# A graph kernel's last stretch in another order: preparation in four sorts instead of five, layers begun two sorts sooner, row fetches put behind the tails' scatters

## The chip, the cores and the metric

The kernel runs on one core of a Trainium2 chip. Its time is the device time of one execution in microseconds. Of the kernel before, nine executions were timed; a tenth was profiled, and that one gives the trace from which all durations are taken.

The engines are TensorE (matmuls; PE in the profile, PEld its weight loads), VectorE (DVE), ScalarE (ACT), GpSimd (POOL) and SyncE (SP). Each works through its own queue in the order in which the program issued it. Transfers are issued from SP's and POOL's queues.

## The reference

Sixteen graphs of 1024 nodes, 64 channels each, and a 0/1 adjacency. Two layers, each on a layer norm, each added to `x`:

```python
# layer 0: h = max(layernorm(x), 0)
skip = jnp.maximum(jnp.where(nb > 10, (nb + 1) // 2, 1), 1)
rem = neigh & (sk > 1) & (rank % sk == sk - 1) & mask[:, :, None]
rem = rem | jnp.swapaxes(rem, 1, 2)
nd = jnp.where(rem, 0.0, adj_) > 0
s = jnp.sort(jnp.where(nd[..., None], x[:, None, :, :], jnp.inf), axis=2)
agg = sum of 0.25, 0.5, 0.25 times the quantiles 0.25, 0.5, 0.75 of s   # per node and channel
out = x + agg; y = relu(out @ W1 + b1) @ W2 + b2                        # masked, x + y
# layer 1: h = max(layernorm(x), 0)
x1 = bn(relu(adj @ (h @ W) + b))      # three times, x1, x2, x3
x + relu(concat([x1, x2, x3]) @ Wl + bl)
```

So each node's remaining neighbours are sorted channel by channel, three weighted quantiles make its aggregate, and then come three products with the whole adjacency.

## The kernel before, in words

The graphs are worked in eight pairs, `p` = 0 to 7. The 1024 nodes of a graph are ordered by their number of neighbours and cut into blocks, so that every block has a sorting network of its own length.

**Blocks.** Three wide blocks (0, 1, 2 in `BLOCKS`, called so here) are gathered on TensorE (`gather_block`: VectorE makes one-hot selections `s`, L1245, TensorE multiplies them with the features into `pg`, L1270, ScalarE copies the result to `g`, L1274) and sorted by `sort_block`. The middle block (`MID`, nodes 960 to 1008) is gathered in the same way and sorted by `sort_pairs`, for two pairs in one network. The last sixteen nodes of each graph, the tails, are sorted for four pairs at once (`TAILS`: after pair 4's turn, and for pairs 4 to 7 in the late part). Three blocks of nodes (`NODES`: 17, 19 and 21 neighbour slots) are sorted by `sort_nodes`. Their rows are not gathered by products: `fetch_nodes` fetches them from `rows_d`, one slot of one graph at a time, with an indirect transfer from POOL's queue (`ask`, L1486), followed after the second graph's by a small memset on POOL (L1498, a "rest"). The first graph's fetch also waits until the sort at that place has gone on. The first and second node block are fetched for one pair, the third for two pairs; `NODE_ORDER` is the order of these jobs. Their buffer, tag "gn", exists once; two late jobs have buffers of their own.

All the sorts are VectorE's compare steps (L1186), the weights and sums follow at L1198 and L1207. The aggregates go to HBM (`agg_d`) by indirect transfers from POOL's queue (`scatter`, L1368).

**Preparation.** `prepare(p)` works out which neighbours remain: ScalarE's and TensorE's passes over the adjacency; `above` and `place` (L975); POOL's scatters to `live_d` (L983) and their load `lp` (L998); ScalarE's `liveT` and `listed` (L1063); then VectorE's `top` (L779, eight neighbours at a time), `rows_listed` (L799), `z` and the features `hp` (L764 to 767). It is done for the second graph after the first.

**Weaving.** The order on the engines is written out: `weave(sort, others...)` runs a sort's generator and steps the others when their share of the sort is passed. `asking(job, first, end, share)` spreads a share of a job's fetches over a stretch of the sort; what is left is issued when that job's sort begins (`ask.rest()`). `steps(n)` gives out `SHARES[n]` steps of the preparation, or in the late part `LATE_SHARES[n]` steps of `later`. A generator that is done simply takes no more steps.

In the loop, the turn of pair `p` has five sorts with preparation of pair `p + 1` beside them: block 0, a job of nodes, block 1, block 2, and one more job of nodes. Then come the middle block of `p` and `p + 1`, with block 0 of `p + 1` gathered beside it, and the next turn. After pair 6's turn the late part sorts pair 7: block 0, a job of nodes (the third node block of pairs 4 and 5), block 1, block 2, the next job of nodes, the tails, a job of nodes, the middle block of pair 7, and three jobs of nodes.

**Layers.** `later` runs the second part of every pair beside the late sorts. `load(p)` (SP, L1693 to 1702) loads `x`, `h`, the aggregates and the mask; the aggregates' load waits for all scatters to that pair's `agg_d`. `first` adds the aggregates (L1594), multiplies by the two weight matrices (`pm` L1603, `py` L1607) and makes the layer norm (`agg`, L624 to 632). `second` loads the transposed adjacency (`adjT`, L1715, two of 1 MB) and runs the three graph layers: the weights' product (`xw`, L1636 to 1642), the product with the adjacency in 96 matmuls (`pg`, L1652), `xT` (L1656), the output's product `pf` (L1668) and the result (L1672 to 1677). In

```python
        loaded = load(p + 1)
        for _ in range(5):
            now.step()
            yield
        ahead = Steps(first(*loaded))
        while now.step():
            yield
            if ahead is not None and ahead.step():
                yield
```

the next pair's load is issued, five more steps of the present pair are taken, and then its first layer alternates with the present pair's steps. `done.sent` says up to which pair the scatters have been issued; `load` may go no further.

Of the kernel before, what the change touches and what calls it, by code (L numbers as in the profile page):

```python
# [30 lines left out]
TAUS = ((0.25, 0.25), (0.5, 0.5), (0.75, 0.25))  # L31

SHARES = (20, 22, 14, 30, 9)
LATE_SHARES = (8, 8, 8, 8, 9, 9, 10, 8, 11, 8, 8)

MAGIC = 8388608.0

# [372 lines left out]
def graph_layers_kernel(ctx: ExitStack, tc: tile.TileContext, ins, out: bass.AP):  # L410
# [6 lines left out]
    NP = NB // 2  # L417
# [1108 lines left out]
    def asking(fetched, first, end, share=1.0):  # L1526

        return fetched[4], math.ceil(share * NODES[fetched[1]][3]), first, end
# [151 lines left out]
    def later(pools, keep, done):  # L1680
# [41 lines left out]
        for p in range(NP):  # L1722
            now = Steps(second(p, *given))
            now.step()
            yield
            ahead = None
            if p + 1 < NP:
                loaded = load(p + 1)
                for _ in range(5):
                    now.step()  # L1730
                    yield
                ahead = Steps(first(*loaded))
# [4 lines that stand above are left out]
            if ahead is not None:  # L1737
                ahead.rest()
                given = ahead.result
# [146 lines left out]
    with ExitStack() as stack:  # L1886
# [6 lines left out]
        with ExitStack() as inner:  # L1893
# [11 lines left out]
            def fetch_next(tag="gn"):  # L1905
                pairs, i = next(jobs)
                return fetch_nodes([sts[p] for p in pairs], i, pools, tag)
# [5 lines left out]
            for p in range(NP - 1):  # L1913
                st = sts[p]
                ahead = Steps(prepare(p + 1, early))

                def steps(n):
                    return ahead, SHARES[n], 0.0, 1.0

                weave(sort_block(st, 0, pools), gather_block(st, 1, pools), asking(nodes, 0.0, 0.9), steps(0))  # L1920
                weave(sort_nodes(nodes, pools), gather_block(st, 2, pools), steps(1))
                nodes = fetch_next()
                weave(sort_block(st, 1, pools), asking(nodes, 0.1, 1.0, 0.4), steps(2))
                send_nodes()
                both = rows_of_pairs(MID, p, p + 1, p, pools, "g1")
                weave(
                    sort_block(st, 2, pools), gather_block(st, MID, pools, into=both),
                    gather_block(st, MID + 1, pools, (early[0], "a", 2)), asking(nodes, 0.0, 0.7), steps(3),
                )
                if p in TAILS:  # L1930
                    tails = rows_of_pairs(MID + 1, *TAILS[p], TAILS[p][1], pools, "g0")
                weave(sort_nodes(nodes, pools), steps(4))
                ahead.rest()
                sts.append(ahead.result)
                nodes = fetch_next()
                if p in TAILS:
                    weave(sort_pairs(MID + 1, *TAILS[p], tails, pools))
                    send(pools)
                weave(
                    sort_pairs(MID, p, p + 1, both, pools), gather_block(sts[-1], 0, pools, first=0.3, end=1.0),  # L1940
                    asking(nodes, 0.0, 1.0, 0.4),
                )


        with ExitStack() as inner:
# [5 lines left out]
            def steps(n):  # L1951
                return ahead, LATE_SHARES[n], 0.0, 1.0

            st = sts[-1]
            weave(sort_block(st, 0, pools), gather_block(st, 1, pools), asking(nodes, 0.0, 0.9), steps(0))
            weave(sort_nodes(nodes, pools), gather_block(st, 2, pools), steps(1))
            nodes = fetch_next()
            then = [fetch_next("r0")]
            weave(sort_block(st, 1, pools), asking(nodes, 0.0, 0.9), steps(2))
            send_nodes()  # L1960
            both = rows_of_pairs(MID, NP - 1, NP, NP - 1, pools, "g1")
            weave(
                sort_block(st, 2, pools), gather_block(st, MID, pools, into=both), asking(then[0], 0.0, 0.9), steps(3)
            )
            tails = rows_of_pairs(MID + 1, *TAILS[NP - 1], NP - 1, pools, "g0")
            weave(sort_nodes(nodes, pools), gather_block(st, MID + 1, pools, into=tails[:, :, -TW:]), steps(4))
            then += [fetch_next(), fetch_next("s"), fetch_next("s")]
            weave(
                sort_pairs(MID + 1, *TAILS[NP - 1], tails, pools), asking(then[1], 0.0, 0.9), steps(5),
            )  # L1970
            send(pools)
            sent_ahead[0] = last_sent[0]
            done.sent = NP - 2
            weave(sort_nodes(then[0], pools), asking(then[2], 0.1, 1.0, 0.6), steps(6))
            send_nodes()
            weave(sort_pairs(MID, NP - 1, NP, both, pools), asking(then[2], 0.0, 0.8), asking(then[3], 0.8, 1.0, 0.1), steps(7))
            send(pools)
            weave(sort_nodes(then[1], pools), asking(then[3], 0.0, 1.0, 0.5), steps(8))
            send_nodes()
            done.sent = NP - 1  # L1980
            weave(sort_nodes(then[2], pools), asking(then[3], 0.0, 0.9), steps(9))
            send_nodes()
            weave(sort_nodes(then[3], pools), steps(10))
            send(pools)
            done.sent = NP
            ahead.rest()
# [49 lines left out]
```

## Time and profile before

| | us |
|---|---|
| median of 9 executions | 2853.47 |
| lowest, highest | 2831.88, 2862.99 |
| profiled execution | 2835.27 |
| its span | 2833.5 |
| VectorE busy in it | 2343.4 (83%) |
| TensorE busy | 2149.8 (76%) |
| POOL busy | 1710.0 (60%) |
| ScalarE busy | 1619.8 (57%) |

The page gives each engine's busy time, its busy share in 40 slices of the span (a digit is tenths), and the costliest groups of instructions: line, engine, operation, tiles, count, then busy time, mean nanoseconds of one, and the idle time ahead of them with what ended it. Beside it the trace was asked for stretches of the span: for each its length, then each engine's busy time with the number of instructions in brackets, the clock that TensorE was granted, the share of the transfer engines and GB/s. In the timeline a line has start, duration, engine, line, operation, tiles, number of instructions, and in square brackets the idle time before it and what ended it. A stall is read from that bracket, not from the busy share.

The last sorts lie in the span as follows, each ending where the next begins: second node block of pair 5, 2051.6 to 2087.8; middle block of pairs 6 and 7, with what follows it, to 2153.2; block 0 of pair 7 to 2196.9; third node block of pairs 4 and 5 to 2246.1; block 1 to 2285.5; block 2 to 2343.9; first node block of pair 6 to 2409.6; tails to 2484.5; then second node block of pair 6 (fetched earlier into its own buffer) to 2563.9; middle block of pair 7 to 2603.1; third node block of pairs 6 and 7 to 2652.2; the two node jobs of pair 7 to 2685.2 and 2726.3. The layers alone go on to 2833.5.

### The profile page before, as it was taken

To read this page: it belongs to the slowest core of one execution; us is meant where nothing else is said; L and a number is where in the kernel's file an instruction comes from. 1 tells how busy PE (TensorE), PEld (TensorE's weight loads), DVE (VectorE), ACT (ScalarE), POOL (GpSimd) and SP (SyncE) were. 2 spreads that over 40 slices of the span, in tenths; PEclk is the share of its full clock that TensorE was granted. 3 is DMA by queue.
4 is the path that set the end of the run, shared out by engine and by line. 5 is a ranking of instruction groups with operands and counts; after the bars stand their busy time and mean duration, and the time that the engine had idled before them with its cause. 6 is when DMAs were issued, how large, how long until landed. Compare 5 with 4: busy or idle time off the path is not lost. (4 is left out here: it accounts for less than half of the span.)

```text
span 2833.5 us, 54810 instructions
## 1 busy us (share of the span) xinstructions
PE 2149.8 (76%) x21204; PEld 1383.0 (49%) x21220; DVE 2343.4 (83%) x5452; ACT 1619.8 (57%) x3255; POOL 1710.0 (60%) x1570
## 2 busy tenths in 40 slices
PE   4658976796689578868975588679758998748888
PEld 2425544454455445545652355445535555425555
DVE  6358988798899888898979998889886987949963
ACT  4564768476758666686767267667672332303322
POOL 7225764575838673865476748674867288888300
PEclk9869977897799789978986799789978988869999
DMA  5114122222322132314152032132213135213221
GB/s 157 53 45 134 59 74 67 87 64 69 76 83 78 56 83 74 90 53 124 55 84 60 21 107 89 47 96 74 80 48 76 22 77 92 60 33 75 70 61 46
DMA packets 262765, 205.43 MB, mean 73 GB/s; under 512 B 218720, under 2 KB 219104, under 8 KB 258400
## 3 DMA queue, kind: packets, MB, share of 16 engines
q1 hardware_dynamic: 178528, 133.61, 16.1%
q0 software_dynamic: 40960, 62.37, 8.9%
q10 hardware_dynamic: 43008, 5.87, 1.8%
q8 instruction: 168, 2.75, 0.4%
q14 instruction: 101, 0.83, 0.1%
HBM read 148.89 MB, written 52.81 MB: 71 GB/s over the span
## 5 line engine op out<-in xcount | busy, mean ns | idle before, releaser
L1486 POOL DMA_INDIRECT g_nodes<-rows_d,rows_listed x744 | 969.2, 1303 | 713.9 <-DVE prod L1198 260.3
L1270 PE MATMUL pg<-s,hp 128*64 128x496 fp8e4 (+5 forms) x8064 | 753.9, 338 | 146.6 <-DVE s L1245 51.1
L1270 PEld LDWEIGHTS <-hp 128*64 128x64 bf16 x8064 | 458.2, 114 | 385.6 <-ACT hp L764 60.7
L1498 POOL MEMSET rest_row<- 1x768 bf16 x372 | 288.7, 776 | 0.1
L1652 PE MATMUL pg<-adjT,xw 128*64 128x512 fp8e4 x2304 | 280.5, 393 | 9.2 <-ACT xw L1637 5.2
L1245 DVE TENSOR_SCALAR s<-r 128x3200 uint16<-128x3200 uint16 (+2 forms) x192 | 206.9, 1086 | 64.4 <-PE pg L1270 49.0
L983 POOL DMA_INDIRECT live_d<-edge,place x128 | 162.9, 1273 | 127.1 <-DVE place L975 64.5
L1274 ACT ACTIVATE g<-pg 128x400 f32<-128x400 f32 (+3 forms) x168 | 83.9, 499 | 224.2 <-PE pg L1270 150.6
L1652 PEld LDWEIGHTS <-xw 128*64 128x64 bf16 x2304 | 135.0, 113 | 138.9 <-issue 24.1
L850 ACT ACTIVATE edge<-a 128x1024 fp8e4<-128x1024 uint32 x128 | 135.4, 1058 | 99.7 <-DMA a<-in_adj 96.5
L942 ACT ACTIVATE edge<-q,bias 128x1024 fp8e4<-128x1024 f32 x128 | 141.9, 1110 | 59.4 <-PE q L937 55.0
L915 ACT ACTIVATE stays<-cs,back 128x1024 f16<-128x1024 f32 x128 | 138.7, 1113 | 58.2 <-PE cs L911 29.0
L1186 DVE TENSOR_TENSOR t<-g 128x800 f32<-128x800 f32 (+9 forms) x184 | 168.0, 926 | 2.4 <-ACT g L1274 0.4
L1018 PE MATMUL pt<-ident_h,lp 128*128 128x128 bf16 x1024 | 106.8, 274 | 81.2 <-ACT liveT L1024 38.3
L1341 PE MATMUL pg<-s,hp 128*64 128x384 bf16 (+14 forms) x1872 | 152.7, 303 | 14.3 <-DVE s L1310 10.9
L1186 DVE TENSOR_TENSOR g<-t 128x992 f32<-128x992 f32 (+7 forms) x176 | 160.0, 934 | 2.3
L1186 DVE TENSOR_TENSOR t_nodes<-g_nodes 128x256 f32<-128x256 f32 (+6 forms) x192 | 124.5, 658 | 42.5 <-DMA g_nodes<-rows_d,rows_listed 28.6
L969 ACT ACTIVATE stays<-keys,minus 128x1024 fp8e4<-128x1024 f32 x120 | 134.0, 1117 | 43.2 <-PE keys L954 27.7
L1368 POOL DMA_INDIRECT agg_d<-o,node_of x96 | 134.5, 1401 | 28.9 <-issue 25.5
L1310 DVE TENSOR_SCALAR s<-r 128x192 bf16<-128x192 bf16 (+11 forms) x544 | 115.2, 302 | 41.1 <-remote 29.8
L857 PE MATMUL ptE<-ident_h,one 128*128 128x128 bf16 x1024 | 83.8, 231 | 81.0 <-DVE one L854 59.8
L1018 PEld LDWEIGHTS <-lp 128*128 128x128 fp8e4 x1024 | 92.0, 126 | 93.7 <-issue 79.6
(272 smaller groups left out, 5116.4 us busy)
## 6 DMA issues: line engine op xcount, KB each, us to landing
a<-in_adj SPq DMA_DIRECT2D x128, 512.0 KB
lp<-live_d POOLq DMA_DIRECT2D x32, 514.0 KB
adjT_d<-edgeT SPq DMA_DIRECT2D x16, 1024.0 KB
adjT<-adjT_d SPq DMA_DIRECT2D x16, 1024.0 KB
g_nodes<-rows_d,rows_listed POOLq DMA_INDIRECT x744
room<-in_x SPq DMA_DIRECT2D x16, 256.0 KB
h_again<-h_d SPq DMA_DIRECT2D x16, 256.0 KB
xt<-in_x SPq DMA_DIRECT2D x16, 256.0 KB
```

What stands on the lines that cost most here:

```text
L850: nc.scalar.activation(edge[:, t, :N], a[:, :].bitcast(U32), AF.Sign, accum_out=found[:, 0, b, t : t + 1], saturate=False)
L915: nc.scalar.activation(stays[:, t, :], cs, AF.Abs, bias=back[:, t : t + 1], scale=2.0)
L942: nc.scalar.activation(edge[:, t, :N], q, AF.Relu, bias=bias(-2.0), accum_out=nv[:, t : t + 1], saturate=False)
L983: sent = nc.gpsimd.indirect_dma_start(out=live_d[b][:, :], out_offset=bass.IndirectOffsetOnAxis(ap=place[:, t : t + 1], axis=0), in_=edge[ ...
L1018: nc.tensor.matmul(out=pt[:, u, :], lhsT=lp[:, u * P : (u + 1) * P], rhs=ident_h, start=True, stop=True)
L1186: sorted_by[0] = nc.vector.tensor_tensor(view(bufs, o, n1, n2), view(bufs, a, n1, n2), view(bufs, b, n1, n2), ALU.max if op else ALU.min)
L1245: nc.vector.tensor_scalar(s[:, j, :, us, :], st.r[0][:, :, us, j0:j1], abs(k - 3), 0x0808, ALU.logical_shift_right if k > 3 else ALU.logic ...
L1270: summed = nc.tensor.matmul(out=pg[x * C : (x + 1) * C, those, :], lhsT=st.hp[:, part, x, u, :], rhs=picked, start=(i == 0 and part == 0), ...
L1341: summed = nc.tensor.matmul(out=pg[x * C : (x + 1) * C, ks, w0:], lhsT=st.hp[:, part, x, u, :], rhs=s[:, ks, x, u, w0:], start=(whole and ...
L1486: asked = nc.gpsimd.indirect_dma_start(out=g[:, k, a * C : (a + 1) * C], out_offset=None, in_=rows_d[st.p][:, :], in_offset=bass.IndirectO ...
L1498: rested[0] = nc.gpsimd.memset(rest_row, 0.0)
L1652: nc.tensor.matmul(out=pg[cs, :], lhsT=part[:, u, cs], rhs=adjT[x][:, u, sl], start=(u == 0 and k == 0), stop=(u == NT - 1 and k == len(xw ...
```

## The change: what it does

The instructions are the same on every engine, in number and kind. From pair 6's turn on they stand in another order.

- In the turn of pair 6 the 95 steps of preparation go beside four sorts (`LAST_SHARES`), and none beside its fifth sort and the middle block after it; these two leave the loop and stand at the head of the late part, with 6 and 5 steps of the layers beside them. `LATE_SHARES` has 13 entries instead of 11.
- `first(p + 1)` starts after two instead of five more steps of the present pair.
- The third node block of pairs 6 and 7 (`then[1]`): only 0.3 of its fetches are put beside the tails' sort, the rest beside the sort after it, and so behind the tails' scatters in POOL's queue. The fetches of the two jobs after it move back likewise.

```diff
@@ -31,7 +31,8 @@
 TAUS = ((0.25, 0.25), (0.5, 0.5), (0.75, 0.25))
 
 SHARES = (20, 22, 14, 30, 9)
-LATE_SHARES = (8, 8, 8, 8, 9, 9, 10, 8, 11, 8, 8)
+LAST_SHARES = (24, 26, 17, 30)
+LATE_SHARES = (6, 5, 6, 6, 6, 6, 6, 7, 10, 8, 11, 8, 8)
 
 MAGIC = 8388608.0
 
@@ -1726,7 +1727,7 @@
             ahead = None
             if p + 1 < NP:
                 loaded = load(p + 1)
-                for _ in range(5):
+                for _ in range(2):
                     now.step()
                     yield
                 ahead = Steps(first(*loaded))
@@ -1915,7 +1916,7 @@
                 ahead = Steps(prepare(p + 1, early))
 
                 def steps(n):
-                    return ahead, SHARES[n], 0.0, 1.0
+                    return ahead, (SHARES if p < NP - 2 else LAST_SHARES)[n], 0.0, 1.0
 
                 weave(sort_block(st, 0, pools), gather_block(st, 1, pools), asking(nodes, 0.0, 0.9), steps(0))
                 weave(sort_nodes(nodes, pools), gather_block(st, 2, pools), steps(1))
@@ -1929,6 +1930,10 @@
                 )
                 if p in TAILS:
                     tails = rows_of_pairs(MID + 1, *TAILS[p], TAILS[p][1], pools, "g0")
+                if p == NP - 2:
+                    ahead.rest()
+                    sts.append(ahead.result)
+                    break
                 weave(sort_nodes(nodes, pools), steps(4))
                 ahead.rest()
                 sts.append(ahead.result)
@@ -1952,35 +1957,41 @@
                 return ahead, LATE_SHARES[n], 0.0, 1.0
 
             st = sts[-1]
-            weave(sort_block(st, 0, pools), gather_block(st, 1, pools), asking(nodes, 0.0, 0.9), steps(0))
-            weave(sort_nodes(nodes, pools), gather_block(st, 2, pools), steps(1))
+            weave(sort_nodes(nodes, pools), steps(0))
+            nodes = fetch_next()
+            weave(
+                sort_pairs(MID, NP - 2, NP - 1, both, pools), gather_block(st, 0, pools, first=0.3, end=1.0),
+                asking(nodes, 0.0, 1.0, 0.4), steps(1),
+            )
+            weave(sort_block(st, 0, pools), gather_block(st, 1, pools), asking(nodes, 0.0, 0.9), steps(2))
+            weave(sort_nodes(nodes, pools), gather_block(st, 2, pools), steps(3))
             nodes = fetch_next()
             then = [fetch_next("r0")]
-            weave(sort_block(st, 1, pools), asking(nodes, 0.0, 0.9), steps(2))
+            weave(sort_block(st, 1, pools), asking(nodes, 0.0, 0.9), steps(4))
             send_nodes()
             both = rows_of_pairs(MID, NP - 1, NP, NP - 1, pools, "g1")
             weave(
-                sort_block(st, 2, pools), gather_block(st, MID, pools, into=both), asking(then[0], 0.0, 0.9), steps(3)
+                sort_block(st, 2, pools), gather_block(st, MID, pools, into=both), asking(then[0], 0.0, 0.9), steps(5)
             )
             tails = rows_of_pairs(MID + 1, *TAILS[NP - 1], NP - 1, pools, "g0")
-            weave(sort_nodes(nodes, pools), gather_block(st, MID + 1, pools, into=tails[:, :, -TW:]), steps(4))
+            weave(sort_nodes(nodes, pools), gather_block(st, MID + 1, pools, into=tails[:, :, -TW:]), steps(6))
             then += [fetch_next(), fetch_next("s"), fetch_next("s")]
             weave(
-                sort_pairs(MID + 1, *TAILS[NP - 1], tails, pools), asking(then[1], 0.0, 0.9), steps(5),
+                sort_pairs(MID + 1, *TAILS[NP - 1], tails, pools), asking(then[1], 0.0, 0.9, 0.3), steps(7),
             )
             send(pools)
             sent_ahead[0] = last_sent[0]
             done.sent = NP - 2
-            weave(sort_nodes(then[0], pools), asking(then[2], 0.1, 1.0, 0.6), steps(6))
+            weave(sort_nodes(then[0], pools), asking(then[1], 0.1, 1.0), steps(8))
             send_nodes()
-            weave(sort_pairs(MID, NP - 1, NP, both, pools), asking(then[2], 0.0, 0.8), asking(then[3], 0.8, 1.0, 0.1), steps(7))
+            weave(sort_pairs(MID, NP - 1, NP, both, pools), asking(then[2], 0.0, 1.0, 0.6), steps(9))
             send(pools)
-            weave(sort_nodes(then[1], pools), asking(then[3], 0.0, 1.0, 0.5), steps(8))
+            weave(sort_nodes(then[1], pools), asking(then[2], 0.0, 0.5), asking(then[3], 0.5, 1.0, 0.3), steps(10))
             send_nodes()
             done.sent = NP - 1
-            weave(sort_nodes(then[2], pools), asking(then[3], 0.0, 0.9), steps(9))
+            weave(sort_nodes(then[2], pools), asking(then[3], 0.0, 0.9), steps(11))
             send_nodes()
-            weave(sort_nodes(then[3], pools), steps(10))
+            weave(sort_nodes(then[3], pools), steps(12))
             send(pools)
             done.sent = NP
             ahead.rest()
```

## The prediction

> **What bounds the kernel now.** I read the page first, then the stretches of the last 830 us sort by sort, then the waits, and last the timeline around each place that the change touches.
>
> ```profile
> span 2833.5 us, 54810 instructions
> DVE  6358988798899888898979998889886987949963
> POOL 7225764575838673865476748674867288888300
> L1486 POOL DMA_INDIRECT g_nodes<-rows_d,rows_listed x744 | 969.2, 1303 | 713.9 <-DVE prod L1198 260.3
> L1498 POOL MEMSET rest_row<- 1x768 bf16 x372 | 288.7, 776 | 0.1
> ```
>
> VectorE sorts and sets the pace nearly everywhere. The exception is the 4 in its row of slices, five from the end: there VectorE idles while POOL stands at 8. A fetch of rows costs POOL 1.303 us busy, and 0.30 us stands ahead of nearly every one that follows another fetch, so 1.6 us; a rest costs 0.776 + 0.16 = 0.94 us. Sort by sort (length, then PE, PEld, DVE, ACT, POOL busy):
>
> ```profile
> 2051.60:2087.80 36.20, 21.43 (x177) 12.31 (x174) 30.37 (x77) 23.53 (x33) 16.31 (x15) 0.64 0.23 73
> 2087.80:2153.20 65.40, 41.67 (x425) 25.47 (x427) 49.15 (x175) 44.74 (x105) 59.52 (x51) 0.80 0.37 88
> 2153.20:2196.90 43.70, 38.26 (x384) 26.95 (x380) 33.51 (x43) 7.86 (x18) 24.61 (x20) 0.92 0.09 16
> 2285.50:2343.90 58.40, 56.79 (x507) 37.44 (x505) 56.87 (x81) 14.69 (x25) 52.30 (x44) 0.98 0.40 91
> 2343.90:2409.60 65.70, 56.71 (x429) 36.57 (x425) 46.74 (x115) 20.53 (x58) 52.85 (x46) 0.82 0.60 96
> 2409.60:2484.50 74.90, 56.98 (x434) 35.54 (x430) 73.19 (x227) 23.91 (x58) 67.33 (x61) 0.89 0.25 66
> 2484.50:2563.90 79.40, 39.54 (x270) 21.92 (x271) 37.43 (x81) 12.99 (x28) 67.31 (x70) 0.72 0.14 23
> 2726.30:2833.50 107.20, 96.33 (x802) 58.45 (x796) 37.77 (x52) 26.74 (x44) 2.41 (x2) 0.97 0.15 41
> ```
>
> The first two are the last sorts of the loop (second node block of pair 5, middle block of pairs 6 and 7). The tails' sort ends at 2484.5; in the next, VectorE works 37.43 of 79.40 us. After the last sort come 107.2 us in which TensorE (96.33) finishes the layers. The waits of the stretch from 2484.5 say what VectorE lacks, and the timeline says why:
>
> ```profile
> DVE agg L1594 <- issue: 36.3, 1, 36.3
> ```
> ```profile
> 2523.52 0.94 POOL L1486 DMA_INDIRECT g_nodes<-rows_d,rows_listed  x1 [0.30 <-issue]
> 2524.77 0.87 POOL L1368 DMA_INDIRECT agg_d<-o_tails,node_of  x1 [0.31 <-issue]
> 2532.39 1.22 DVE L1594 TENSOR_TENSOR agg<-agg,h_late 128x1024 f32<-128x1024 f32 x1 [36.27 <-issue]
> ```
>
> Pair 4's first layer waits for the aggregates that the tails' scatters write, and the scatters stand in POOL's queue behind fetches: POOL, 40 us late, holds VectorE for 36.3 us. The start of that queue is where the change works first:
>
> ```profile
> 2047.97 0.17 DVE L975 TENSOR_SCALAR place<-above 128x8 int32<-128x8 f32 x1 [0.34 <-issue]
> 2100.77 0.75 DVE L779 MAX8 top<-listed 128x8 f32<-128x256 f32 x2 [1.74 <-ACT listed L1063]
> 2085.30 1.08 POOL L1486 DMA_INDIRECT g_nodes<-rows_d,rows_listed  x1 [14.40 <-DVE t_nodes L1186]
> 2186.41 1.49 DVE L1186 TENSOR_TENSOR t_nodes<-g_nodes 128x1280 f32<-128x1280 f32 x1 [9.81 <-DMA g_nodes<-rows_d,rows_listed]
> 2725.25 10.75 PE L1652 MATMUL pg<-adjT,xw 128*64 128x512 fp8e4 x96
> ```
>
> The second graph's neighbours are listed 53 us after its places are known; 42 fetches start when the node sort has released its buffer (2085.3), and 101 us later VectorE still waits 9.8 us for the last of them.
>
> **The change part by part.** No instruction comes or goes: TensorE, VectorE, ScalarE, POOL and SP issue what they issued, in another order. What counts is what each place waits for now.
>
> *Preparation in four sorts; start of the fetches.* Pair 7's listing (`top` to `hp`, 73 VectorE instructions, 17.8 us) ran inside the pairs' sort of 65.4 us; now it must end with the node sort before it. It cannot start before `listed`, and as VectorE works in order, the sort behind it waits along. The first graph's scatters to `live_d` stand behind 19 fetches of their sort instead of 24, 5 x 1.6 = 8 us sooner, so `place` of the second graph comes at about 2040. From there to `listed` POOL's 11 more scatters, two loads and ScalarE's `liveT` took 53 us here and 45 in two earlier turns; I take 49: 2089 instead of 2100. The 17.8 us of listing, of which a few are done beside the wait, and about 10 of sort and `hp` follow: the node sort ends near 2115, and its buffer is released 24 us later than before, at 2109. Bounds: +15 (45 us, listing half hidden) and +37 (`listed` no sooner than before and everything after it).
>
> *From there to the end of the third node block of pairs 4 and 5* (2246.1 before). The same 42 fetches, with 6 scatters among them instead of 8 (2 x 1.4 = 3 us less). VectorE is no cover lost: between the two places it worked 49.2 + 33.5 of 109.1 us, and the listing's 17.8 are gone from it, so it waits for the fetches as it did, 9.8 us before, more now. Behind the last fetch 7 layer instructions fewer stand (17 instead of 24), at 0.7 to 1.2 us each 7 us. **+24 - 3 - 7 = +14 us** (+5 to +27). The layer steps given to the loop's last two sorts (16 VectorE instructions) are paid here, in sorts that wait anyway: no cost of their own, up to 10 us if the wait is gone.
>
> *From there to the tails' scatters* (2524.8, 278.7 us). POOL is the bound: it had no break over 4 us in it. After the change 113 fetches stand in it where 128 stood, since 15 of the third block's fetches move behind the scatters; rests 71 for 72, scatters 14 in both. 15 x 1.6 + 0.9 = 25, and of the 4.0 us break (at 2405.6) I take 3 as gone, as VectorE comes sooner: **-28 us**. Bounds: -18 (15 x 0.95 + 0.30 = 1.25 us each, the pace of the line at 2523.52) and -36 (with the one fetch of 8.6 us too). The wait for the aggregates therefore does not go: VectorE too gets there sooner, by the 16 to 18 layer instructions already done and fewer waits in the sorts from 2285.5 on. I expect 25 to 33 us of the 36.3 to remain.
>
> *The scatters themselves.* Pair 4's two were first and second of eight; now first and seventh. Five more at 1.14 us each (0.84 + 0.30 in this block): **+6 us** (0 to +9).
>
> *From pair 4's first layer to the last sort's end* (2532.4 to 2726.3, 193.9 us, VectorE full but for short breaks). Between the two, 24 VectorE instructions fewer stand in the queue, as the layers are at another place: at the stage's mean 0.45 us that is 11, at 0.68, as a layer's, 16; I take **-13**. Against it: 69 fetches instead of 54 stand behind the scatters, 24 us of POOL. The cover is POOL's idle time there, 22.5 us ahead of the scatter at 2685.6 and about 18 in the sort before it; it just suffices. SP's queue is crossed too: the load of the next pair's aggregates, which waits for the third block's scatters, now stands ahead of the load of `adjT`. Without cover these give up to 13 back: -17 to 0.
>
> Together the last sort ends at 14 - 28 + 6 - 13 = **21 us sooner, near 2705.**
>
> *The tail.* The layers give up their lead: at the tails' sort 108 of their VectorE instructions are done where 111 were, at the last sort 206 where 212 were. Pair 6's last product began 1.05 us before the last sort ended (2725.25); now pair 5's third layer still stands there, as the first layer of the next pair is pulled ahead of it by three steps: one `pg` pass of 10.75 us, about half of an output product of 5.62, the weights' product 2: **+15 us** on the 107.2, in which TensorE is 96.33 busy and hides nothing. Bounds +6 (half runs in VectorE's gaps) and +22 (the loads of `adjT` late as well).
>
> Sum: **-6 us**. The profiled execution took 2835.27 around its span of 2833.5, so it would take 2829; against the median of 2853.47, which lies 0.64% above that execution, **2847 us**. The five terms' bounds, taken as independent, make +-18 us; eight in ten within +-13.
>
> [...] Fetches take 0.95 us busy where VectorE idles (2523.52) and 1.303 in the mean. [...]
>
> **The rivals.**
> *The stall goes.* If the listing ends with the sort at 2100 (+5 instead of +14), the fetches keep 1.25 to 1.6 us and the tail grows by 8 only: 5 - 30 + 6 - 14 + 8 = -25, 2828 us. For it: the idle 65 - 49 us of VectorE in the pairs' sort. Against: the chain to `listed` was 45 us or more in every turn.
> *The layers fall behind (slower).* The tail takes pair 5's third layer, +15 to +22, and POOL pays the sooner scatters back in the two sorts after them, so that the last sort ends where it did: 2869 to 2875, say 2871. It decides from the point where the last sort gains under the tail's 15 us, and is over 0.5% once it gains under 1. For it: TensorE 96.33 of 107.2, and the cover of the 24 us is used up. Against: 15 fetches did leave the path.
> *Nothing moves*: POOL's total is the same and the fetches only change places, 2853.
>
> **How the numbers follow.** Forecast 0.45, the stall goes 0.27, the layers fall behind 0.23, nothing 0.05. 0.5% is 14 us (2839 and 2868), about what can be told from no change. The forecast's own range 2834 to 2860 gives 0.13 faster, 0.31 same, 0.01 slower; the first rival 0.25 and 0.02; the second 0.02 same, 0.21 slower; the third 0.05 same. Faster 0.38, same 0.40, slower 0.22. Range: 2820 to 2872, from the first rival less 8 to the second.
>
> **What would show it.** Right: 42 fetches starting near 2109, that block's end near 2260, the first tails' scatter near 2510, a wait of 25 to 33 us at `agg`, the last sort's end near 2705, a tail of some 122. Wrong: `listed` no sooner than 2100; POOL waiting between loop end and tails' scatters, so that asks weren't the bound; VectorE waiting for rows in the last two sorts; a tail under 113.

## The result and the profile after

The changed kernel is slower: 2909.06 us in the median (2895.24 to 2927.64) against 2849.72 for the kernel before (2824.86 to 2875.1), ratio 1.0219 with a 95% interval of 1.0191 to 1.0247. Forecast was 2847, with 2820 to 2872 as the range. The two profiled executions lie further apart than the medians, 2919.93 against 2835.27 us.

The page of the changed kernel, and its sorts by stretches with the columns of before:

```profile
span 2918.2 us, 54787 instructions
DVE  6358988788888979889989997896897987847852
POOL 7234856484828655773857666738474687977200
L1487 POOL DMA_INDIRECT g_nodes<-rows_d,rows_listed x744 | 1004.1, 1350 | 763.3 <-DVE prod L1199 273.4
```
```profile
2090.30:2138.40 48.10, 22.42 (x197) 13.55 (x198) 45.71 (x137) 36.89 (x63) 5.52 (x1) 0.75 0.06 12
2397.30:2453.20 55.90, 36.18 (x320) 24.76 (x319) 37.49 (x84) 14.64 (x44) 36.61 (x30) 0.88 0.51 84
2453.20:2518.30 65.10, 37.38 (x268) 23.88 (x265) 64.10 (x216) 17.09 (x48) 61.10 (x39) 0.78 0.17 51
2518.30:2607.40 89.10, 39.44 (x259) 22.83 (x260) 37.42 (x80) 12.88 (x29) 71.41 (x72) 0.68 0.18 34
2790.30:2918.20 127.90, 112.17 (x906) 71.52 (x902) 41.71 (x59) 29.15 (x47) 1.97 (x2) 0.96 0.19 55
```

VectorE's work is the same (2342.8 us), its dip five slices from the end is still there. The loop's last node sort takes 48.1 us for 36.2, the tail 127.9 for 107.2. POOL, which was expected to be the bound between loop and tails' scatters, works only 36.61 of 55.9 us in the first node block of pair 6. The wait at the first layer of pair 4, from the list of waits in 2518.3 to 2607.4, has grown:

```profile
DVE agg L1595 <- DMA agg<-agg_d: 44.8, 1, 44.8
```

And the timeline at the places that the prediction named:

```profile
2111.67 0.75 DVE L780 MAX8 top<-listed 128x8 f32<-128x256 f32 x2 [2.25 <-ACT listed L1064]
2132.88 10.81 POOL L1487 DMA_INDIRECT g_nodes<-rows_d,rows_listed  x1 [52.53 <-DVE t_nodes L1187]
2231.16 1.49 DVE L1187 TENSOR_TENSOR t_nodes<-g_nodes 128x1280 f32<-128x1280 f32 x1 [20.35 <-DMA g_nodes<-rows_d,rows_listed]
2429.56 0.69 DVE L1643 TENSOR_TENSOR xw<-rest,xw 128x512 bf16<-128x512 f32 x1 [12.83 <-ACT none L1331]
2447.69 2.06 POOL L1487 DMA_INDIRECT g_nodes<-rows_d,rows_listed  x1 [12.45 <-DVE prod L1199]
2570.70 0.87 POOL L1369 DMA_INDIRECT agg_d<-o_tails,node_of  x1 [0.30 <-issue]
```

The 42 fetches start 47.6 us later than before, VectorE waits 20 us for the last of them, later 12.8 us behind ScalarE, and POOL then 12.5 us behind VectorE. The first tails' scatter comes 45.9 us later instead of 15 sooner. Two of the signs that were named for a wrong forecast are there: the second graph's listing begins no sooner than 2100 (at 2111.7), and POOL waits between the loop's end and the tails' scatters.

Cut at the five places of the prediction, the profiles give this. The first row goes to the end of the second sort of pair 6's turn; at the end of the sorts that the change leaves alone, two sorts earlier, its two numbers are +7.9 and -5.2. The last column sets the whole change against the fetches' part alone on two chips of like pace (runs e5_again and e13_fetch2 below), so it is what the first two parts cost.

| | forecast | after less before | whole change less fetches' part |
|---|---|---|---|
| ahead of block 1's sort in pair 6's turn | 0 | +10.9 | -2.9 |
| to the end of the third node block of pairs 4 and 5 | +14 | +29.8 | +23.7 |
| from there to the first tails' scatter | -28 | +5.2 | +15.1 |
| from there to pair 4's first layer | +6 | +7.2 | +2.5 |
| from there to the last sort's end | -13 | +10.9 | +7.7 |
| the tail | +15 | +20.7 | +17.8 |
| sum | -6 | +84.7 | +63.9 |

### The profile page after: what moved, and what is told of

Read it like the earlier page. It is cut to its first block, busy times and chain, and to the rows that moved or that the text cites. A ratio compares the mean times of both kernels' runs of the same rounds, so it can differ in the third digit from the quotient of the medians.

```text
span 2918.2 us, 54787 instructions
## 1 busy us (share of the span) xinstructions
PE 2173.2 (74%) x21204; PEld 1399.2 (48%) x21220; DVE 2342.8 (80%) x5452; ACT 1620.0 (56%) x3255; POOL 1737.4 (60%) x1570
## 5 line engine op out<-in xcount | busy, mean ns | idle before, releaser
L1487 POOL DMA_INDIRECT g_nodes<-rows_d,rows_listed x744 | 1004.1, 1350 | 763.3 <-DVE prod L1199 273.4
L1271 PE MATMUL pg<-s,hp 128*64 128x496 fp8e4 (+5 forms) x8064 | 765.2, 339 | 153.9 <-DVE s L1246 53.2
L1653 PE MATMUL pg<-adjT,xw 128*64 128x512 fp8e4 x2304 | 289.3, 400 | 14.6 <-issue 6.3
L984 POOL DMA_INDIRECT live_d<-edge,place x128 | 157.0, 1227 | 124.7 <-DVE place L976 63.3
L1653 PEld LDWEIGHTS <-xw 128*64 128x64 bf16 x2304 | 143.0, 115 | 144.6 <-issue 41.4
L970 ACT ACTIVATE stays<-keys,minus 128x1024 fp8e4<-128x1024 f32 x120 | 134.1, 1118 | 44.8 <-PE keys L955 27.0
L1657 ACT ACTIVATE xT<-pg,c_L_gnn_b 128x512 f32<-128x512 f32 x48 | 32.8, 684 | 198.0 <-PE pg L1653 161.5
```

The source lines that it names most:

```text
L984: sent = nc.gpsimd.indirect_dma_start(out=live_d[b][:, :], out_offset=bass.IndirectOffsetOnAxis(ap=place[:, t : t + 1], axis=0), in_=edge[ ...
L1271: summed = nc.tensor.matmul(out=pg[x * C : (x + 1) * C, those, :], lhsT=st.hp[:, part, x, u, :], rhs=picked, start=(i == 0 and part == 0), ...
L1487: asked = nc.gpsimd.indirect_dma_start(out=g[:, k, a * C : (a + 1) * C], out_offset=None, in_=rows_d[st.p][:, :], in_offset=bass.IndirectO ...
L1653: nc.tensor.matmul(out=pg[cs, :], lhsT=part[:, u, cs], rhs=adjT[x][:, u, sl], start=(u == 0 and k == 0), stop=(u == NT - 1 and k == len(xw ...
```

## The experiments

**Each part alone.** The four kernels ran on one chip, whose median for the kernel before is 2774.97.

Only the fetches (the last hunks of the diff):

```diff
-                sort_pairs(MID + 1, *TAILS[NP - 1], tails, pools), asking(then[1], 0.0, 0.9), steps(5),
+                sort_pairs(MID + 1, *TAILS[NP - 1], tails, pools), asking(then[1], 0.0, 0.9, 0.3), steps(5),
...
-            weave(sort_nodes(then[0], pools), asking(then[2], 0.1, 1.0, 0.6), steps(6))
+            weave(sort_nodes(then[0], pools), asking(then[1], 0.1, 1.0), steps(6))
...
```

> Only the third part of the change: the fetches of the third node block of pairs 6 and 7 move behind the tails' scatters; preparation stays in five sorts, the layers' shares and the five steps stay. Theory (the loss comes from the preparation in four sorts, the fetches are not to blame): 15 fetches at 1.6 us leave POOL's queue ahead of the scatters, the first tails' scatter comes near 2502 instead of 2524.8, the wait at the first layer of pair 4 falls from 36 to about 15 us, and the kernel is 5 to 20 us faster than before. Rival (the fetches that moved back hold up the later sorts): VectorE waits for rows in the last three sorts, and the kernel is 5 to 20 us slower.

2753.74 us, ratio 0.9916 (0.9888 to 0.9945): faster. The stretch to the tails' scatters is 262.1 us (267.1 and 263.6 in two later profiles of the same kernel), 12 to 17 shorter than in the profile of before, and the wait at pair 4's first layer 21.8 us. The tail is unchanged, 107.0.

Only the sooner first layer:

```diff
-                for _ in range(5):
+                for _ in range(2):
                     now.step()
```

> Only the second part: the next pair's first layer begins after two instead of five more steps. Theory: the tail is what it touches, a part of pair 5's third layer slips behind the last sort: +5 to +15 us, all of it after the last sort's end. Rival (the order of SP's loads holds up the layers beside the sorts): the same or more, but lost before the last sort's end. Second rival: nothing, within 5 us.

2793.33 us, ratio 1.0074 (1.0045 to 1.0104). The tail is 115.0, so 8 us are lost there; the rest is lost earlier, and the longest waits there are not for SP's loads. In the first node block's sort of pair 6 (list of waits, 2269 to 2345):

```profile
ACT o L1389 <- DMA agg_d<-o,node_of: 29.8, 1, 29.8
DVE xT L1657 <- ACT xT L1656: 24.1, 2, 23.6
```

`o` is the buffer from which a block's aggregates are scattered. There are three; the fourth copy on ScalarE waits for the first scatter, the scatter stands in POOL's queue behind fetches, and VectorE's next layer step stands behind ScalarE. In the kernel before that copy waited 2.0 us. A layer step that comes sooner comes to this place before POOL does.

Preparation in four sorts with the layers begun sooner, fetches and five steps as before (first and last hunks of the diff without the `range` and `asking` lines):

> Only the first part: preparation in four sorts and the layers begun beside the loop's last two sorts with the new shares; fetches and the five steps as before. Theory (preparation in four sorts loses the time): the sort of block 2 in the last turn starts some 25 us late, the node sort after it ends some 38 us late, and the kernel is 35 to 65 us slower, the larger part of the whole change's 59. Rival (it is the three together, or the other two): within 15 us of before.

2819.31 us, ratio 1.0161 (1.0122 to 1.0199). Counted from the sorts ahead of it, and against the first profile of before, block 2's sort starts 15 us late (25 were expected), the node sort after it ends 27 us late (38 expected). The tail is 120.8.

The same without layer steps in the loop's last two sorts:

```diff
-LATE_SHARES = (6, 5, 6, 6, 6, 6, 6, 7, 10, 8, 11, 8, 8)
+LATE_SHARES = (0, 0, 8, 8, 8, 8, 9, 9, 10, 8, 11, 8, 8)
```

> Preparation in four sorts alone: the last two sorts of the loop have no steps of the layers beside them, the later shares, the fetches and the five steps are those of before. Theory: as slow as the kernel with the layers begun sooner, within 10 us, since the delay arises in the preparation and the layer steps lie beside waits. Rival (the layer steps put in the two sorts hold up the listing, TensorE and ScalarE being in order): 15 us or more faster than that kernel, and the node sort after block 2 ends 10 us sooner than there.

2801.95 us, ratio 1.0091 (1.0054 to 1.0127). So preparation in four sorts costs 27 us and the layers 17 more, against the theory; but the rival's reason is not it either, since the node sort ends 28 us late here too. The layer steps pay at the third node block (it ends 10 us late with them, 24 without), and lose the same in the tail (120.8 against 106.4). In between, the stretch from the third node block to the tails' scatters takes 304.7 us with them and 289.2 without, so that the scatters come no sooner: POOL's fetches take 9 us longer (189.0 for 179.9, 129 each), VectorE's longest wait in the sort before the tails' is 21.0 for 10.4 us, and POOL's longest wait for a fetch buffer, first with the layer steps, then without:

```profile
POOL g_nodes L1487 <- DVE prod L1199: 10.8, 1, 10.8
```
```profile
POOL g_nodes L1487 <- DVE prod L1199: 3.9, 1, 3.9
```

The two kernels differ in `LATE_SHARES` alone and ran on one chip, so this is shown by an edit: layer steps that come sooner make this stretch longer, in VectorE and in POOL. Where the 17 us of the medians arise is open; the two profiled executions lie only 6 us apart (2811.34 and 2805.57).

**Do the parts add up?** On a chip with 2770.67 for before:

> The changed kernel once more, on the chip on which its parts are measured. The three parts alone gave 1.6%, 0.7% and -0.8%. Theory (the parts add up): 1.5% slower, and no wait of ScalarE of 7 us before block 2's sort nor of VectorE of 11 us in the third node block's sort, which only that one profile showed. Rival (the third part loses its gain beside the others): 2.0 to 2.5% slower, as measured before.

2813.38 us, ratio 1.0166 (1.0126 to 1.0206). The parts alone give 1.61 + 0.74 - 0.84 = 1.5%: they add up. The two long waits named there are absent. The interval of the first measurement (from 1.0191) just meets this one (to 1.0206); what it may owe to its chip comes below.

Without the fetches' part:

> The changed kernel with the fetches where they were: first and second part together. Theory (parts add up): 2.3% slower, and the fetches' part is worth 0.8% here too. Rival (first and second part let VectorE run into POOL sooner, so that what the fetches' order gains is lost in other waits): 1.5 to 2.2% slower, no more than 0.3% from the changed kernel.

2834.24 us, ratio 1.0235 (1.0193 to 1.0277). So the fetches' part is worth 0.7% beside the others too: the first tails' scatter comes 303.8 us after the third node block without it and 282.1 with it. From the lists of waits of this kernel, and of the changed one on the same chip:

```profile
DVE agg L1595 <- DMA agg<-agg_d: 67.8, 1, 67.8
```
```profile
DVE agg L1595 <- DMA agg<-agg_d: 46.7, 1, 46.7
```

An edit of the preparation's shares:

```diff
-LAST_SHARES = (24, 26, 17, 30)
+LAST_SHARES = (24, 26, 6, 41)
```

> The changed kernel with the preparation's steps in its last turn given as 24, 26, 6 and 41 instead of 24, 26, 17 and 30: at the end of block 1's sort 56 steps are out, as in the kernel before. Theory (the chain of the second graph, put ahead of the last gather of block 2 on TensorE and ScalarE, delays that sort): block 2's sort starts within 5 us of the kernel before, 15 to 25 us sooner than in the changed kernel, the node sort after it ends as late as there or up to 10 us sooner since it waits for the listing, and the kernel is 0 to 15 us faster than the changed one. Rival (the listing is only pushed back): the node sort ends 10 us or more later than in the changed kernel, and the kernel is 10 us or more slower.

2814.86 us, ratio 1.0173. The edit left the order of the instructions as it was: in the traces it is the same on VectorE, POOL and SP, and on ScalarE and TensorE a few neighbours at one place are exchanged. So it tells nothing of the theory and only repeats the changed kernel. That the second graph's chain ahead of the last gather delays block 2's sort is therefore read from the trace, not shown by an edit.

**Is POOL's queue the bound?** Fetches' part, and no rests in the late part (`done` is made where the late part begins):

```diff
+    resting = [True]
...
-                    if a == G - 1:
+                    if a == G - 1 and resting[0]:
...
             done.sent = 4
+            resting[0] = False
```

> The fetches' part alone, and in the late part no rests between the fetches: some 92 memsets of 0.94 us leave POOL's queue, 73 of them between the third node block of pairs 4 and 5 and the tails' scatters. Theory (POOL's queue is what sets the end): the tails' scatters come 40 to 65 us sooner, the wait at the first layer of pair 4 goes, and the kernel is another 15 to 35 us faster than with the fetches' part alone, that is 1.4 to 2.1% faster than before. Rival (the rests pace the transfers, without them the fetches take longer): a fetch takes 0.3 us or more longer in the mean, and the kernel is within 10 us of the fetches' part alone, or slower.

2710.43 us, ratio 0.9802 (0.9761 to 0.9843), faster than both kernels. The stretch to the tails' scatters is 237.2 us, the wait at the first layer of pair 4 is gone. On the two chips that ran the fetches' part with and without these rests (below), the stretch is 31 and 28 us shorter without them, while the 73 rests in it took POOL 54 us. So POOL's queue sets much of the length of this stretch, but not all of it. Four more kernels, no rests in the late part of the changed kernel, half of a block's fetches put later in it, no rests in the late part of the kernel before, and none in the whole kernel with the fetches' part, ran together on a chip with 2864.05 for before:

> The changed kernel without rests between the fetches of the late part. Theory (in the changed kernel VectorE runs into POOL's queue, at the copies for block 2's scatters and at the first layer of pair 4; what is left without that is a later loop end, some 20 us, and a longer tail, some 18): both waits go, the kernel is 60 to 90 us faster than the changed one, and still 25 to 45 us slower than the fetches' part without rests, so 0.3 to 1.0% faster than before. Rival (with POOL out of the way the sooner layers pay): as fast as the fetches' part without rests, 1.6 to 2.2% faster than before, or faster still.

> The changed kernel with half of the fetches of pair 6's second node block put one sort later; in POOL's queue 8 fetches come behind the first four of block 2's scatters. Theory (VectorE and POOL wait for each other in turn: the copy to a buffer of the scatters waits for the scatter before, VectorE stands behind it, releases the fetch buffer late, and POOL then waits for that): the wait of VectorE in the first node block's sort of pair 6 falls from 15 to under 7 us, POOL's wait for the buffer from 10 to under 4, and the tails' scatters come 5 to 12 us sooner; the kernel is 5 to 12 us faster than the changed one. Rival (POOL's work alone sets the time of the tails' scatters): both waits fall, but the tails' scatters come within 3 us of where they were, and the wait at the first layer of pair 4 takes the difference.

```diff
-                sort_block(st, 2, pools), gather_block(st, MID, pools, into=both), asking(then[0], 0.0, 0.9), steps(5)
+                sort_block(st, 2, pools), gather_block(st, MID, pools, into=both), asking(then[0], 0.0, 0.9, 0.5), steps(5)
...
-            weave(sort_nodes(nodes, pools), gather_block(st, MID + 1, pools, into=tails[:, :, -TW:]), steps(6))
+            weave(sort_nodes(nodes, pools), gather_block(st, MID + 1, pools, into=tails[:, :, -TW:]), asking(then[0], 0.0, 0.9), steps(6))
```

> The kernel before, without rests in the late part. Theory (POOL's queue was the bound of that stretch, and either fewer fetches or fewer rests relieve it): the wait of 36 us at the first layer of pair 4 goes, 1.2 to 2.0% faster; the fetches' part is then worth 0.4% at most. Rival (the two gains add, since they act at different places): 1.0 to 1.3% faster.

> The fetches' part and no rests in the whole kernel. Theory (in the loop VectorE sets the pace, but the listing waits for scatters that stand behind fetches and rests): 5 to 40 us faster than without rests in the late part alone, 2.1 to 3.4% faster than before. Rival (the rests in the loop let transfers of the preparation through): slower than without rests in the late part alone by 5 us or more.

Ratios: 1.0185 (1.0098 to 1.0273), 1.0198 (1.0109 to 1.0287), 1.0153 (1.005 to 1.0256) and 1.0959 (1.0866 to 1.1053). The first three meet neither of their expectations, the last its rival, far beyond the size that was given. The waits did go: without rests the one at pair 4's first layer is 1.2 us in the changed kernel and none in the kernel before, and yet both lose. The timeline shows why. TensorE in the kernel before without rests, beside POOL at the same time:

```profile
2302.82 0.58 PE L1653 MATMUL pg<-adjT,xw 128*64 128x512 fp8e4 x1 [2.22 <-issue]
2305.62 0.58 PE L1653 MATMUL pg<-adjT,xw 128*64 128x512 fp8e4 x1 [2.22 <-issue]
2308.42 0.58 PE L1653 MATMUL pg<-adjT,xw 128*64 128x512 fp8e4 x1 [2.22 <-issue]
```
```profile
2303.64 0.94 POOL L1486 DMA_INDIRECT g_nodes<-rows_d,rows_listed  x1 [0.30 <-issue]
2304.88 0.95 POOL L1486 DMA_INDIRECT g_nodes<-rows_d,rows_listed  x1 [0.31 <-issue]
2306.14 0.95 POOL L1486 DMA_INDIRECT g_nodes<-rows_d,rows_listed  x1 [0.30 <-issue]
```

One matmul each 2.8 us with no wait shown, while POOL sends a fetch each 1.25 us. In the run with the fetches put later it is one each 1.41 us beside fetches and scatters; the changed kernel on the chip of 2770.67 runs the same pass in one piece:

```profile
2349.25 11.02 PE L1653 MATMUL pg<-adjT,xw 128*64 128x512 fp8e4 x81
```

The run with the fetches put later therefore does not decide on the turns that VectorE and POOL take: the copy to `o` waited 3.9 us instead of 13.8 and VectorE behind it 4.6 instead of 12.8, but 18 us were lost a step later for such matmuls, POOL waited 14.9 us for its buffer, and the scatters came 287 us after the third node block, not sooner.

**Chip or kernel?** The same programs on another chip (2765.25 for before):

> The fetches' part alone once more, on another chip. Theory (its gain is POOL's shorter queue ahead of the tails' scatters, on any chip): 0.4 to 1.2% faster. Rival (on a chip on which TensorE lacks instructions beside fetches the gain is lost): within 0.4% or slower.

> The fetches' part without rests in the late part once more. Theory (the chip decides): 1.5 to 2.4% faster where TensorE's idle time with nothing shown stays under 5 us, 0.5 to 2.5% slower where it is 60 us or more. Rival (it is the fetches' order that makes the rests superfluous, on any chip): 1.5 to 2.4% faster in either case.

> The kernel before without rests in the late part once more. Theory (the chip decides): where TensorE does not lack instructions, 1.2 to 2.0% faster, the wait at the first layer of pair 4 gone; where it does, 1 to 2% slower as before. Rival (without the fetches' part the rests are needed on any chip): slower in either case.

What these expectations call lacking instructions is the idle time ahead of TensorE's matmuls for which nothing is shown, 2.22 us at a time in the timeline above; that instructions were what was missing is not shown. Ratios 0.9928 (0.9903 to 0.9953), 0.9820 (0.9778 to 0.9862) and 0.9865 (0.9824 to 0.9906). The kernel before without rests is 1.35% faster here (17.1 us of the wait at pair 4's first layer remain) and 1.5% slower there, with the same program. The group of the adjacency product on the page, first there, then here:

```profile
L1653 PE MATMUL pg<-adjT,xw 128*64 128x512 fp8e4 x2304 | 302.6, 400 | 85.1 <-issue 59.4
```
```profile
L1653 PE MATMUL pg<-adjT,xw 128*64 128x512 fp8e4 x2304 | 275.8, 389 | 5.5 <-ACT xw L1642 2.8
```

So it is not the kernel alone. It is the chip, or something else that went with it, as none of the chips on record was used a second time. In what follows the first kind is a chip like the one there (before at 2840 us or more) and the second kind one like the one here (some 2770). Summing the idle stretches over 0.7 us ahead of matmuls for which nothing is shown gives 32 us for the first profile of before, 50 for the changed kernel, 64 with the fetches put later, 100 to 102 without rests in the late part, 201 without any, and 0 to 2 us in every profile from a chip on which the kernel before takes some 2770. It is not the whole difference: the kernel before without rests spans 2906.9 us there and 2735.4 here, 171 us apart, of which this idle time is 102; its mean granted clock was 0.855 there and 0.879 here. Nor does most of it lie in the late part for the kernel before: the sorts ahead of the change end at 1956.9 us in its first profile and at 1891 to 1906 in the profiles of the second kind whose program is the same up to there.

> The fetches' part alone a third time. Theory: 0.4 to 1.2% faster also where TensorE lacks instructions beside fetches, since there are as many fetches and rests as before. Rival: within 0.4% or slower on such a chip.

> The fetches' part without rests a third time. Theory (the chip decides): 0.5 to 2.5% slower where TensorE's idle time with nothing shown is 60 us or more, 1.5 to 2.4% faster where it stays under 5 us. Rival: faster on either.

Again such a chip (2770.48): ratios 0.9929 (0.9905 to 0.9953) and 0.9794 (0.9757 to 0.9831). Neither version ran on a chip of the first kind; what they do there is open.

> The kernel before, profiled on another chip. Theory (a chip without lacking instructions only shortens stretches that TensorE's waits lengthen): a span near 2770 us, the waits with nothing shown gone from TensorE, and in the last stretch the same order: 36 to 50 us of waiting at the first layer of pair 4, a stretch of 278 to 285 us from the third node block of pairs 4 and 5 to the tails' scatters, a tail of 107. Rival (the chips differ in POOL's pace): that stretch is 10 us or more shorter or longer.

It fell on a chip of the first kind: span 2851.2 us, 33 us of that idle time, and so not near 2770. The stretch to the tails' scatters is 287.7 us where the first profile had 278.7, the wait 45.2 where it had 36.3. Some 10 us of scatter between profiles must be allowed in every term of the table's column "after less before".

## Why the prediction was wrong

Against the first profile of before, the changed kernel on a chip of the second kind (e5_again) has these five terms, from the third node block on: +20.0 (forecast +14), +3.6 (-28), +7.2 (+6), -9.4 (-13) and +17.9 (+15) us, in all 39. The medians on that chip lie 43 us apart. The two profiles come from different kinds of chips, so some 10 us of scatter may lie in each term; one is off by more than that, the second.

*Start of the fetches, +24.* Right, in size and in its steps. Counted from the end of the second sort of pair 6's turn, and with that end laid on the one in the first profile of before, e5_again has the second graph's `place` at 2041 (forecast about 2040), its listing at 2088 (2089), the node sort's end at 2115 (2115) and the first fetch at 2109 (2109). Against the three profiles of the fetches' part alone that is 23 to 28 us later. Block 2's sort starts 15 us late with the preparation in four sorts, as TensorE and ScalarE take the second graph's `stays` and `q` ahead of the last pieces of block 2's gather, which the prediction did not have; but VectorE still waits 4.0 us for the listing when it comes to it, so the chain that was forecast ends last. In the first pair of profiles the fetches start 37 us later: there `place` comes no sooner than before, and VectorE waits 12.6 us before block 2's sort for something that the profile does not name.

*To the end of the third node block, +14.* Measured +20 on the second kind of chip, +24 there against the fetches' part alone, +30 in the first pair. The 3 us for two scatters did not come (a fetch of 10.81 us stands at the head now), the 7 us for fewer layer instructions were 4.

*From there to the tails' scatters, -28: the step that failed.* It measured +3.6, and +5.2 in the first pair. "15 x 1.6 + 0.9 = 25" was nearly right as a part: the fetches' part takes 12 to 17 us off this stretch alone, and 22 beside the other two on one chip. What was wrong is "POOL is the bound", as if the stretch were POOL's work alone, with each fetch at the price that it had. What the first two parts cost POOL here was put at nothing, even at a gain of 3 us. They make the stretch 303.8 us (without the fetches' part) where two profiles of before had 278.7 and 287.7: 14 to 18 us of that are longer fetches. So after the whole change POOL is as long busy with 115 fetches as with 130 before. The groups of the stretch, before and in e5_again:

```profile
L1486 POOL DMA_INDIRECT g_nodes<-rows_d,rows_listed x130 | 169.9, 1307 | 34.3 <-issue 26.0 <-DMA mk<-in_nodemask 4.0 <-DMA g_nodes<-rows_d,rows_listed 1.2
```
```profile
L1487 POOL DMA_INDIRECT g_nodes<-rows_d,rows_listed x115 | 172.1, 1497 | 34.9 <-issue 22.7 <-DVE prod L1199 9.7 <-DMA g_nodes<-rows_d,rows_listed 0.9
```

The waits grow too. Layer steps come sooner to places that need POOL: VectorE waits there (23.6 us in the kernel with only the sooner first layer, 15.3 in the changed one on the same kind of chip), releases the fetch buffer late, and POOL waits for it, 9.7 us for 4. The fetches are longest in the tails' sort. Its groups before, in e5_again, and in the fetches' part alone:

```profile
L1486 POOL DMA_INDIRECT g_nodes<-rows_d,rows_listed x35 | 49.0, 1400 | 7.3 <-issue 6.0 <-DVE g_pairs L1186 0.8 <-DVE xT L1657 0.3
```
```profile
L1487 POOL DMA_INDIRECT g_nodes<-rows_d,rows_listed x20 | 49.0, 2451 | 3.8 <-issue 3.4 <-DVE g_pairs L1187 0.3 <-DVE t_pairs L1187 0.2
```
```profile
L1486 POOL DMA_INDIRECT g_nodes<-rows_d,rows_listed x28 | 52.1, 1859 | 5.1 <-issue 4.2 <-DVE t_pairs L1186 0.6 <-DVE g_pairs L1186 0.3
```

A fetch takes 1.40, 2.45 and 1.86 us there. In the profile of the changed kernel, too, the tails' sort has 20 fetches of 2.45 us in the mean, and the 17 that start while VectorE waits after it (2540.7 to 2570.7) took 0.94 or 0.95 each. What makes a fetch longer in the tails' sort no run shows, nor what the single ones of 9.51 and 9.60 us there are (e5_again, e13_fetch2). The prediction had 0.95 us beside an idle VectorE and 1.303 in the mean, and took 1.6 us off for each of the 15 fetches that moved. One price was too simple: what a fetch costs differed from sort to sort. Buffer wait (6 us more) and longer fetches (10 us more in all) make up the 15 us of the table's last column. That layer steps which come sooner lengthen both is shown by the two kernels that differ in `LATE_SHARES` alone; that the one follows from the other's turn was argued from the trace, and the run made for it did not decide.

*The wait at pair 4's first layer remains, 25 to 33 us.* It grew to 44.8 and 46.7. As said, the wait does not go; its size was taken too small with the step above, since the scatters did not come sooner.

*To the last sort's end, -13.* -9.4 in e5_again and +10.9 in the first pair. The work is as forecast: from pair 4's first layer on, 381 VectorE instructions stand where 405 stood, 24 fewer, and their durations are 14 us shorter in sum. In the first pair the idle time took that back, 32 us for 10; VectorE waited 11.0, 5.1 and 3.4 us ahead of layer steps for something that the profile does not name, waits that no profile of the second kind of chips has. The fetches' part alone takes 16 us off this stretch (177.5 for 193.9), since 28 instructions have moved ahead of the wait; beside the other two parts it takes nothing off (184.5 with it, 184.1 without). The 7.7 us of the last column are 6 us more idle time and 2 of work.

*The tail, +15.* 17.8 and 20.7: right in cause and nearly in size. It is the layers' order: 8 us from the sooner first layer alone, 14 from the layers begun sooner alone, which keeps the forecast's point that a lead given up at the tails' sort comes back in the tail.

The rival that the layers fall behind named the loss in the tail rightly, but its other half, that the last sort's end stays where it was, did not hold: that end is later.

## What to carry to other kernels

Where two engines feed each other through few buffers, a stretch need not be the busier one's work: here layer steps that came sooner went with a wait of POOL for the fetch buffer of 10.8 us instead of 3.9, and with a stretch of 304.7 us instead of 289.2. A mean price per instruction is that of the order in which it was measured: here POOL's fetches in the tails' sort took 49.0 us with 35 of them and with 20. Measure the parts of a change alone: here one part gained 0.7 to 0.8% and was buried under two that lost 2.3%. And compare times on one chip: a wait on "issue" at a steady pace beside another engine's transfers is a reason to run the same program on a second one. Here such waits came to 102 us on one chip and 0 to 2 us on another, with one program.

## What the runs showed of the hardware

Two kinds of chips, or of sessions on them, answer differently to the same program. On the one (before at 2840 to 2864 us) TensorE at places advances by one matmul in 2.80 us, with no wait shown, while POOL issues an indirect transfer each 1.25 us, and in another run by one in 1.41 us; in the profiles from the other (2765 to 2775 us) such idle time is 0 to 2 us. On the first kind it is longer in the runs with fewer memsets between fetches, 32 and 33 us in two profiles of the kernel before and 50 in the changed one, 100 to 102 without those of the late part, and 201 without any and with the fetches' part, where the kernel is 9.6% slower. Without those of the late part, the kernel before is 1.5% slower there and 1.35% faster on the second. What this idle time comes from, no view of the trace shows.
